# A convolution plus quantised feed-forward kernel: the order of the table work in the lead, regrouped

## The chip, the cores and the metric

The kernel runs on one core of a Trainium2 chip. The metric is the device time of one execution in microseconds (us). Before the change it is 1074.47 us, the median of 3 runs (1073.33, 1074.47 and 1075.77). Engines are named as the profile names them: PE is the matrix engine, DVE the vector engine, ACT the scalar (activation) engine, POOL the general engine, SP the engine that issues most DMAs. L12 means line 12 of the kernel before; the changed kernel's lines are told by the same numbers, so that an operation keeps its name.

## The reference, cut to what matters

The input `x` is (32, 64, 1024): 32 sequences, 64 channels, length 1024. One residual layer is computed:

```python
kernel = _get_kernel(log_dt, C, log_A_real, A_imag, Lq)   # 64 channels x 1024 taps
y = irfft(rfft(u_m) * rfft(kernel))[..., :Lq] + u_m * D   # a causal convolution, plus a skip
cond = y * mask                                           # and a length mask
c2 = cond.reshape(32 * 64, 1024)
gate, up = c2 @ Wg, c2 @ Wu                               # weights of 4 bits, dequantised
out = x + ((gate * sigmoid(gate) * up) @ Wd).reshape(x.shape)   # the product in float16
```

`_get_kernel` is `2 Re sum_n Cs[h,n] exp(dtA[h,n] * l)` over 64 modes `n` for each channel `h` and each tap `l`. The feed-forward contracts over the 1024 positions; its rows are the 2048 pairs of a sequence and a channel, and it has 2752 inner units. So a channel's convolution must be done over all positions before its rows can enter the feed-forward.

## The kernel before, in words

**The taps.** The 1024 taps of a channel are the product of two tables of 32 entries: tap `32a + b` is a sum over 128 rows (64 modes, real and imaginary) of `e1[a] * e2[b]`. The coefficients (decay `na`, phase `wh` and `wl`, amplitude `ab`) come first, for channels 0 to 31 (`head_coefficients`, small DVE instructions of 128x32 and 128x64). Then a group of 4 or 8 channels goes through these steps:

- `decay_tables` (L168): one Exp on ACT per channel, 128x64, into `xd`.
- `phase_tables` (L192 to L204): eight DVE instructions (two products, two roundings, four subtractions), then on ACT two Sin (L207) and two Square (L209). Sin and Exp sit in different table sets of ACT, so an ACT_TABLE_LOAD stands between them.
- `kernel_factors` (L218 to L223): five DVE instructions that make `e2` and `e1`.
- `make_kernel` (L425 to L434): matmuls on PE, one per channel, into `kq`; then `kb`, a high part by ACT (L430) and a low part by DVE (L431), both float16; then two DMAs, issued by ACT (L433), that write them to `kpad` in DRAM.
- `toeplitz` (L525): SP loads, per channel, a 512 KB Toeplitz matrix from `kpad` in overlapping rows.

Groups start at channels 0 and 4 (four channels each), 8, 16 and 24 (eight each). This text says "kernel 8" for the taps of the group that starts at channel 8, and `t0[8]` for the Toeplitz matrix of channel 8.

**The convolution.** `conv_head` makes 24 matmuls (L548) per channel: 8 steps, and in each a high-by-high, a high-by-low and a low-by-high product. Its other operand is the input, cut by `conv_split` (or `conv_load` from channel 16 on) into a float16 high part `uh` (ACT, L495 or L507) and a low part `ul` (DVE, L497 or L510), four channels at a time. After two channels DVE multiplies by the mask (L560), ACT rounds the result to `xh` (L563), and POOL (for channel 15 DVE) makes `xl` (L565). A block is 16 channels, 16 * 32 = 512 rows of the feed-forward, which lie along the free dimension.

**The feed-forward.** `gu_one` and `gu_pair` (L664, L665, L687, L688) multiply `xh` and `xl` with the 4-bit weights, which an unpacker (L578, L579 on SP, L584 on DVE, L590 on POOL, L596 on ACT) prepares; after each group of 128 rows the sums in PSUM are rescaled (L618, L620, L637, L640) by ratios that `scale_ratios` made beforehand (L410 to L418). `dn_pair` (L736, L737) does the down projection.

**What sets the order.** Each engine executes its instructions strictly in the order of its own list. That order is made when the kernel is built: a scheduler places instructions by priority and by its own estimates, and `after(key)` adds the rule that what is issued under it comes after a marked instruction. In the first block (`for i, _ in enumerate(c.conv(0))`, L944) a dictionary `events` issues other work at a given step; eight steps make one channel, so step 7 ends channel 0, step 23 channel 2, step 56 begins channel 7 and so on. `busy(h0, n)` issues `n` matmuls (L891) whose result nobody reads. SP's list is one queue: a load that waits holds up all loads behind it. The SP and ACT DMAs use eight completion semaphores in turn, so a DMA also waits for the eighth one before it.

Of the kernel before, what the change touches and what calls it, by code (L numbers as in the profile page):

```python
# [17 lines left out]
ALU = mybir.AluOpType  # L18
# [164 lines left out]
def phase_tables(nc, side, pool, co, cst, h0, nh):  # L183
# [19 lines left out]
    stt(r1, r1, off1, pl, ALU.subtract, ALU.subtract)  # L203
    stt(r2, r2, off2, pl[:, :, 32:], ALU.subtract, ALU.subtract)  # L204
# [5 lines left out]
    return r1, r2, sq_op  # L210

# [47 lines left out]
class Core:  # L259
# [145 lines left out]
    def scale_ratios(self, s16, nt, g, name, last_factor):  # L405
        nc, keep = self.nc, self.keep
        ratio = keep.tile([128, nt, g - 1], F32, name=name + "r")
        last = keep.tile([128, nt], F32, name=name + "l")
        s, z = self.take([128, nt, g], F32), self.take([128, nt, g], F32)
        nc.scalar.copy(s, s16)  # L410
        for t0, t1, p0, p1, f in last_factor:
            nc.scalar.mul(last[p0:p1, t0:t1], s[p0:p1, t0:t1, g - 1], f)
        nc.vector.tensor_scalar(z, s, 0.0, 2.0 ** -60, ALU.is_equal, ALU.mult)
        nc.vector.tensor_tensor(s, s, z, ALU.add)
        for t0 in range(0, nt, 11):
            t1 = min(nt, t0 + 11)
# [25 lines left out]

    def tables(self, pool, h0, nh):
        held = h0 >= 24
        steps = phase_tables(self.nc, self.nc.vector, pool, self.co, self.cst, h0, nh)
        while True:
            try:
                with self.after("dve" if held else None), self.after("act" if held else None):
                    next(steps)
            except StopIteration as done:  # L450
                self.tab, sq_op = done.value[:2], done.value[2]
                break
            self.dve(800)
            yield
# [36 lines left out]

    def conv_split(self, k, after, last="e"):
        u, uh, ul = self.us[k]
        with self.after(("sq", after)):
            self.nc.scalar.copy(uh, u)  # L495
        with self.after((last, after)):
            self.nc.vector.tensor_tensor(ul, u, uh, ALU.subtract)  # L497
        self.us[k] = uh, ul
# [344 lines left out]
def tile_ssm_ffn(ctx, tc, io):  # L843
# [38 lines left out]
    c.taps(kg, 16)  # L882
    xd = [decay_tables(nc, kg, co, c.cst, h0) for h0 in (0, 8)]
    section(steps)
# [7 lines left out]

    for k, h0 in enumerate((0, 4)):
        every(c.tables(tables, h0, 4))
        every(c.factors(kg, h0, 4, xd[0][:, h0:h0 + 4]))
        c.make_kernel(kg, h0, 4, "b")
        for h in range(h0, h0 + 4):
            c.t0[h] = c.toeplitz(h)
        busy(h0, 8 - 4 * k)
        c.conv_split(k, h0)  # L900
    every(c.tables(kg, 8, 8))
    every(c.factors(kg, 8, 8, xd[1]))
    c.masks()
    tc.no_sync_barrier()
# [22 lines left out]
    def kernel_8():  # L927
        c.make_kernel(kg, 8, 8, "b")
        with c.after("act"):
            xd.extend(decay_tables(nc, kg, co, c.cst, h0) for h0 in (16, 24))  # L930
        for k in (2, 3):
            c.conv_split(k, 8, "kb")
        steps = c.tables(kg, 16, 8)
# [8 lines left out]

    events = {7: kernel_8, 63: lambda: busy(4, 10), 56: ratios_gu, 87: load_16, 75: lambda: c.make_kernel(kg, 16, 8, "b")}
    for i, _ in enumerate(c.conv(0)):  # L944
        if i in events:
            with c.after("dve" if i == 56 else None):
                events[i]()
# [179 lines left out]
```

## Time and profile before

| what | value |
|---|---|
| median of 3 runs | 1074.47 us |
| the profiled execution, its own time | 1075.33 us |
| its span, first to last instruction | 1073.5 us |
| around the span (1075.33 - 1073.5) | 1.8 us |
| PE busy | 1026.2 us, 96% of the span |
| DVE, ACT, POOL busy | 803.7, 775.6, 246.5 us |
| first convolution matmul (L548) starts | 24.53 us |
| last matmul of the first block ends | 58.46 us |
| first feed-forward matmul (L664) starts | 62.15 us |
| DMA, mean | 93 GB/s over the span, 261 GB/s over the first 65 us |

The profile is one execution on the chip. Its second part cuts the span in 40 slices of 26.8 us and gives busy tenths; its fourth follows the chain of waits back from the last instruction; the timeline lists instructions in order of their start, with the idle time of the engine before them and what ended it. "Landed" is the time at which a DMA's semaphore told that it was done. The lead, the subject here, is the first 65 us of 1073.5.

### The profile page before, as it was taken

The page shows a single profiled execution, that of the slowest core. Times are in us where ns is not written, and L with a number is a line of the kernel's source. Part 1 is how long each engine was busy: PE and PEld are TensorE (multiplying, and loading weights), DVE is VectorE, ACT ScalarE, POOL GpSimd, SP SyncE. Part 2 cuts the span into 40 slices and gives each one's busy share as a digit, 9 for nine tenths or more (in the row PEclk, how much of TensorE's full clock was granted, in tenths as well). Part 3 has the DMA queues.
Part 4 walks back from the last instruction along what each step waited for, and adds up shares of the span by engine and source line. Part 5 has one row for each costly group of instructions (what it writes and reads, how often), then busy time and mean ns, then how long its engine had stood idle before and what let it go on. Part 6 is the DMA issues. An engine that isn't in the chain of part 4 may idle for free.

```text
span 1073.5 us, 15382 instructions
## 1 busy us (share of the span) xinstructions
PE 1026.2 (96%) x5854; PEld 513.5 (48%) x5854; DVE 803.7 (75%) x939; ACT 775.6 (72%) x1034; POOL 246.5 (23%) x270
## 2 busy tenths in 40 slices
PE   3989999999999999997999999999999999999996
PEld 2867444444344445663665444444444444444442
DVE  8965788888977786768446777777877777777776
ACT  5767777787677777777577777666666667878775
POOL 0333233232332242231103112221111222102102
PEclk9999999999999999999999999999999999999998
DMA  6976321111111534546753001000000001424102
GB/s 197 331 244 211 101 69 40 40 59 40 42 48 50 143 88 156 164 156 196 231 167 128 30 29 51 20 13 17 20 20 20 20 20 58 129 79 148 59 1 79
DMA packets 52099, 99.76 MB, mean 93 GB/s; under 512 B 9524, under 2 KB 11444, under 8 KB 52024
## 3 DMA queue, kind: packets, MB, share of 16 engines
q1 hardware_dynamic: 38888, 70.09, 20.8%
q0 software_dynamic: 5280, 17.31, 4.3%
q10 hardware_dynamic: 7856, 11.37, 3.6%
q8 instruction: 46, 0.75, 0.3%
q14 instruction: 29, 0.24, 0.1%
HBM read 78.99 MB, written 19.76 MB: 92 GB/s over the span
## 4 chain that ended last, share of the span: by engine, by line
PE 83%; ACT 5%; DMA 4%; DVE 4%; issue 2%; POOL 0%; SPq 0%; DVEq 0%; ACTq 0%
PE chq L687 23%; PE chq L688 22%; PE chq L736 13%; PE chq L737 13%; PE cq L548 6%; PE chq L664 2%; PE chq L665 2%; DMA t<-kpad 2%; ACT chq L640 1%; DVE chq L618 1%; ACT chq L620 1%; DVE v L700 1%; DMA ihl<-kpad 1%; DMA ihl<-xF 1%; PE chq L741 1%
## 5 line engine op out<-in xcount | busy, mean ns | idle before, releaser
L687 PE MATMUL chq<-xh,w 128*128 128x512 f16 x1216 | 460.4, 380 | 5.7 <-DVE chq L618 2.1
L688 PE MATMUL chq<-xl,w 128*128 128x512 f16 x1216 | 458.6, 380 | 0.0
L618 DVE TENSOR_SCALAR chq<-chq,gur 128x1024 f32<-128x1024 f32 x261 | 333.2, 1289 | 95.3 <-PE chq L688 94.1
L620 ACT ACTIVATE chq<-chq,gur 128x1024 f32<-128x1024 f32 x285 | 304.3, 1085 | 86.8 <-PE chq L688 85.5
L640 ACT ACTIVATE chq<-chq,dnr 128x512 f32<-128x512 f32 x372 | 242.1, 661 | 71.7 <-PE chq L737 63.8
L736 PE MATMUL chq<-ihl,wd 128*128 128x512 f16 x672 | 253.8, 380 | 6.5 <-ACT chq L640 3.5
L737 PE MATMUL chq<-ihl,wd 128*128 128x512 f16 x672 | 253.4, 380 | 0.0
L637 DVE TENSOR_TENSOR chq<-chq,dnr 128x1024 f32<-128x1024 f32 x129 | 158.4, 1231 | 83.6 <-PE chq L737 83.2
L688 PEld LDWEIGHTS <-w 128*128 128x128 fp8e4 x1216 | 118.9, 98 | 155.3 <-issue 19.4
L687 PEld LDWEIGHTS <-w 128*128 128x128 fp8e4 x1216 | 118.9, 98 | 145.9 <-issue 1.9
L310 POOL TENSOR_TENSOR ihl<-v,ihl 128x512 f16<-128x512 f32 x42 | 48.3, 1150 | 362.9 <-ACT ihl L629 362.9
L737 PEld LDWEIGHTS <-wd 128*128 128x128 fp8e4 x672 | 65.5, 98 | 76.0 <-issue 12.7
L548 PEld LDWEIGHTS <-t 128*128 128x128 f16 x1152 | 81.4, 98 | 39.2 <-DMA t<-kpad 5.9
L736 PEld LDWEIGHTS <-wd 128*128 128x128 fp8e4 x672 | 65.7, 98 | 67.7 <-issue 1.7
L548 PE MATMUL cq<-uh,t 128*128 128x256 f16 (+3 forms) x720 | 91.8, 226 | 4.6 <-DMA t<-kpad 4.5
L565 POOL TENSOR_TENSOR xl<-y,xh 128x512 f16<-128x512 f32 x28 | 36.2, 1294 | 161.5 <-ACT xh L563 161.5
L548 PE MATMUL cq<-ul,t 128*128 128x256 f16 (+3 forms) x360 | 71.6, 225 | 0.0
L629 ACT CAST ihl<-v 128x512 f16<-128x512 f32 x42 | 25.9, 617 | 58.7 <-DVE v L700 55.3
L700 DVE SCALAR_TENSOR_TENSOR v<-chq,gul,sg 128x1024 f32<-128x1024 f32 x38 | 48.6, 1280 | 17.1 <-PE chq L688 11.3
L310 POOL TENSOR_TENSOR spill<-v,spill 128x512 f16<-128x512 f32 x42 | 48.8, 1161 | 14.2 <-ACT spill L629 13.9
L640 ACT ACTIVATE chq<-chq,gur 128x512 f32<-128x512 f32 x66 | 43.2, 661 | 11.0 <-PE chq L665 9.8
L590 POOL TENSOR_TENSOR w<-w,z 128x256 int32<-128x256 int32 x42 | 31.5, 770 | 82.0 <-DVE w L584 77.6
(250 smaller groups left out, 820.5 us busy)
## 6 DMA issues: line engine op xcount, KB each, us to landing
t<-kpad SPq DMA_DIRECT2D x48, 512.0 KB, 4.4
spill<-spill POOLq DMA_DIRECT2D x42, 256.0 KB, 2.7
ihl<-spill ACTq DMA_DIRECT2D x42, 256.0 KB, 2.8
z<-zc SPq DMA_DIRECT2D x29, 256.0 KB, 3.7
u<-xF SPq DMA_DIRECT2D x12, 512.0 KB, 3.7
xr<-xT SPq DMA_DIRECT2D x12, 512.0 KB, 4.7
out<-xr POOLq DMA_DIRECT2D x24, 256.0 KB, 2.9
w<-qgu SPq DMA_DIRECT2D x21, 256.0 KB, 4.1
```

The costliest lines, as they stand in the source:

```text
L310: self.nc.gpsimd.tensor_tensor(out, a, b, op)
L548: nc.tensor.matmul(q[:, d:, h % 2, :], t0[:, lw, 128 * d:128 * d + 128], uu[:, 0:8 - d, h % 4, :], start=(d == 0 and k == 0 and h % 2 == 0 ...
L565: split.tensor_tensor(xl[:, :, ts], yv, xh[:, :, ts], ALU.subtract)
L618: self.mark("dve", self.nc.vector.tensor_scalar(q, q, col, None, ALU.mult))
L620: self.mark("act", self.nc.scalar.activation(q, q, AF.Copy, scale=col))
L637: self.mark("dve", self.nc.vector.tensor_tensor(q, q, cols.to_broadcast([128, 2, 512]), ALU.mult))
L640: self.mark("act", self.nc.scalar.activation(q[:, k], q[:, k], AF.Copy, scale=cols[:, k]))
L687: nc.tensor.matmul(q[:, b], lw, xh[:, g, :], start=(g == 0), stop=False, skip_group_check=True)
L688: nc.tensor.matmul(q[:, b], lw, xl[:, g, :], start=False, stop=(g == GH - 1), skip_group_check=True)
L700: nc.vector.scalar_tensor_tensor(v, q, last, self.sg.pop(ct - 21), ALU.mult, ALU.mult)
L736: nc.tensor.matmul(qs[j], lw, self.ihl[:, g, 0], start=(g == 0), stop=False, skip_group_check=True)
L737: nc.tensor.matmul(qs[j], lw, self.ihl[:, g, 1], start=False, stop=False, skip_group_check=True)
```

## The change

The diff, cut to its core:

```diff
 # phase_tables also returns the last DVE instruction (L204); tables marks it ("r", h0)
-    def tables(self, pool, h0, nh):
+    def tables(self, pool, h0, nh, key=None):
...
-                with self.after("dve" if held else None), self.after("act" if held else None):
+                with self.after("dve" if held else key), self.after("act" if held else None):
...
+                self.mark(("r", h0), done.value[3])
...
 # scale_ratios
-        nc.scalar.copy(s, s16)
+        with self.after("act"):
+            nc.scalar.copy(s, s16)
...
-    def conv_split(self, k, after, last="e"):
+    def conv_split(self, k, act, dve):
         u, uh, ul = self.us[k]
-        with self.after(("sq", after)):
+        with self.after(act):
             self.nc.scalar.copy(uh, u)
-        with self.after((last, after)):
+        with self.after(dve):
             self.nc.vector.tensor_tensor(ul, u, uh, ALU.subtract)
...
-    xd = [decay_tables(nc, kg, co, c.cst, h0) for h0 in (0, 8)]
+    xd = [decay_tables(nc, kg, co, c.cst, 0)]
...
-    for k, h0 in enumerate((0, 4)):
-        every(c.tables(tables, h0, 4))
+    for h0, fillers in ((0, 8), (4, 2)):
+        every(c.tables(tables, h0, 4, ("e", 0)))
+        if h0 == 0:
+            with c.after(("sq", 0)):
+                xd.append(decay_tables(nc, kg, co, c.cst, 8))
         every(c.factors(kg, h0, 4, xd[0][:, h0:h0 + 4]))
         c.make_kernel(kg, h0, 4, "b")
         for h in range(h0, h0 + 4):
             c.t0[h] = c.toeplitz(h)
-        busy(h0, 8 - 4 * k)
-        c.conv_split(k, h0)
-    every(c.tables(kg, 8, 8))
+        busy(h0, fillers)
+    c.conv_split(0, ("sq", 4), ("e", 4))
+    every(c.tables(kg, 8, 8, ("r", 4)))
+    c.conv_split(1, ("sq", 4), ("r", 8))
     every(c.factors(kg, 8, 8, xd[1]))
-    c.masks()
+    with c.after(("e", 8)):
+        c.masks()
...
     def kernel_8():
         c.make_kernel(kg, 8, 8, "b")
+        for k in (2, 3):
+            c.conv_split(k, "act", ("kb", 8))
         with c.after("act"):
             xd.extend(decay_tables(nc, kg, co, c.cst, h0) for h0 in (16, 24))
-        for k in (2, 3):
-            c.conv_split(k, 8, "kb")
...
-    events = {7: kernel_8, 63: lambda: busy(4, 10), 56: ratios_gu, 87: load_16, 75: lambda: c.make_kernel(kg, 16, 8, "b")}
+    events = {23: kernel_8, 63: lambda: busy(4, 6), 72: ratios_gu, 87: load_16, 66: lambda: c.make_kernel(kg, 16, 8, "b")}
...
-            with c.after("dve" if i == 56 else None):
+            with c.after("dve" if i == 72 else None):
```

In the order that each engine's list takes (read from the two built programs), this does the following. SP's list keeps its order of loads. Behind the first gate-and-up chains, that is from about 80 us of the trace before, all lists are the same.

- DVE: the eight table instructions of group 4 and the first one of group 8 (L192), which stood before the last factor of group 0 (L223), stand behind it; the low parts of the inputs (L497) stand behind the factors of group 4 (channels 0 to 3) and behind the last table instruction of group 8 (channels 4 to 7); the masks (L395, L397, L403) stand behind the factors of group 8; those for channels 8 to 15 behind kernel 8's low part, and the ratios of gate and up (L413 to L418) behind that of kernel 16.
- ACT: eight of the sixteen early Exp move behind the squares of group 0, and with them come one more Exp and one more Sin table load; two input copies (L495) move behind kernel 8's `kb`, and so do the sixteen later Exp, as before; the first of these copies stands between that `kb` and its DMAs. The scale copies (L410, L412) move from before kernel 8's `kb` to behind kernel 16's. One `xh` (L563, channels 0 and 1) stands before kernel 8's `kb`.
- PE: kernel 8's matmuls stand behind channel 2 in place of channel 0; kernel 16's one-channel-per-matmul part (L427) behind the first four matmuls of channel 10 in place of the middle of channel 9; the fillers (L891) number 8, 2 and 6 in place of 8, 4 and 10; the first feed-forward matmul stands behind the first five of channel 17 in place of the seventeenth of channel 16.

More of the change, by code (lines that the diff above doesn't have):

```diff
@@ L203, in phase_tables @@
     stt(r1, r1, off1, pl, ALU.subtract, ALU.subtract)
-    stt(r2, r2, off2, pl[:, :, 32:], ALU.subtract, ALU.subtract)
+    last = stt(r2, r2, off2, pl[:, :, 32:], ALU.subtract, ALU.subtract)
     yield
@@ L209, in phase_tables @@
         sq_op = nc.scalar.activation(r, r, AF.Square, scale=1.4142135623730951)
-    return r1, r2, sq_op
+    return r1, r2, sq_op, last
 def kernel_factors(nc, pool, co, xd, s1, s2, h0, nh):
```

## The prediction

> **What bounds the kernel now.** I read the page's busy rows first, then the busy time in two stretches, before and after 65 us. The columns after the stretch are its length, then the busy time of PE, PEld, DVE, ACT and POOL, the granted clock, the DMA share and GB/s.
>
> ```profile
> 0.00:65.00 65.00, 42.55 (x521) 37.64 (x522) 56.70 (x163) 39.98 (x91) 17.96 (x20) 0.97 0.80 261
> 65.00:1073.50 1008.50, 983.67 (x5336) 475.84 (x5333) 746.97 (x776) 735.59 (x944) 228.51 (x250) 0.99 0.26 82
> ```
>
> Behind the lead PE is busy 97.5% and its list there is not changed. So the change can only move the point from which PE runs full; what it moves there goes to the end one to one. That point is the start of channel 17 at 63.05. The chain of waits up to it (start, length, what):
>
> ```profile
> 10.29 6.90 DMA ihl<-xF
> 17.19 0.29 DVE e1t L223
> ...
> 49.38 0.27 ACT kb L430
> 49.68 0.42 DVE kb L431
> 50.12 5.82 DMA kpad<-kb
> ...
> 56.49 6.50 DMA t<-kpad
> 63.05 0.50 PE cq L548 x3
> ```
>
> Kernel 16's taps are written from 49.67, landed at 55.96, and `t0[17]` landed at 63.0: the last thing that PE waits for. Why `kb` came so late stands in ACT's timeline (start, length; in brackets idle time before):
>
> ```profile
> 30.17 0.36 ACT L430 ACTIVATE kb<-kq 32x256 f16<-32x256 f32 x1
> 30.54 1.28 ACT L168 ACT_TABLE_LOAD   x1
> ...
> 40.87 0.60 ACT L563 CAST xh<-y 128x512 f16<-128x512 f32 x1
> 41.38 2.18 ACT L596 ACTIVATE w<-w,cst 128x1024 fp8e4<-128x1024 uint8 x2
> 46.67 0.62 ACT L563 CAST xh<-y 128x512 f16<-128x512 f32 x1 [3.11 <-DVE y L560]
> 47.20 2.18 ACT L596 ACTIVATE w<-w,cst 128x1024 fp8e4<-128x1024 uint8 x2
> 49.28 0.36 ACT L430 ACTIVATE kb<-kq 32x256 f16<-32x256 f32 x1
> ```
>
> ACT sat 3.11 us for `y` of channels 6 and 7, which on DVE stood behind the ratios, and then did two unpack steps ahead of `kb`. Last, PE in windows of its clock:
>
> ```profile
> 26.13:29.54 3.41, 1.44 (x24) 1.00 0.67 244
> 29.54:32.96 3.42, 3.42 (x29) 0.50 0.83 223
> 56.85:60.27 3.42, 1.61 (x28) 1.00 0.94 248
> ```
>
> After a window with 1.44 us busy the clock was 0.50 for 3.41 us (channels 1 and 2 took 2.76 and 1.92 us; others 1.53, so 1.62 lost); after one with 1.61 it stayed.
>
> **Part by part.** Durations are start-to-start spacings of the rows of before.
>
> Group 0. Nine table instructions leave the way of L223: .34+.34+.26+.20+.33+.20+.39+.26+.60 = 2.92, and L395 .12. They filled gaps of a dependent chain of small instructions; seven such gaps of about .1 open, +.8. Group 0's factor ends at 17.47-3.04+.8 = 15.2; `kb` could follow .73 later (17.47 to 18.20), at 15.95. ACT: squares done at 12.9, then the added Exp load 1.28 and 8 Exp (half of 3.92) 1.96: free at 16.15. So `kb` 0 at 16.2, **-2.0**, and the load of `t0[0]`, 20.46 before, could be issued at 18.5; but input loads run until 18.76 and the write is under them: 18.5 to 19.5, I take 19.0 (-1.5). The fillers stay.
>
> Group 4. Its tables and group 8's first ones now run behind 15.2. DVE: 2.55 for group 4 with `kb`'s low part, 2.47 for five of group 8, 1.9 for the factors: factor end 22.3, before 20.8. ACT: `kb` 16.5, two DMA issues .83, added Sin load 1.28, four functions 1.1: 19.85, in time. Then two input copies 1.98 and a Sin .5: `kb` 4 at 23.0 (22.97 before), its square .5 ahead of the DMAs: written at 23.6 to 23.9, **+.4**. It landed .5 after the queue had run dry (28.5); the queue now runs dry 1.5 earlier, so loads 4 to 7 go at 28.5, before 29.15: **-.6**. The low part of channel 0 (L497) ends at 23.4: channel 0 starts at 23.1, before 24.53. Four fillers less there are free: PE waits.
>
> [...]
>
> Kernel 8. DVE: two low parts 1.13 each, `kb` .2, L204 .4: 25.0; factors 2.05: 27.1, before 28.68. But PE takes channels 1 and 2 first, and ACT has `xh` of channels 0 and 1 ahead of `kb`, which needs the masks (.95) and two tables of group 16 (1.2): `y` 29.05 to 29.75, `xh` 30.35, `kb` 30.4, **+.2**. One input copy (1.0) stands ahead of its DMAs: 31.8, before 30.56, **+1.2**. The wait of PE at 26.76 (1.97) goes. Landing under load took 4.5 (first write of 30.56) to 5.9 (second): loads 8 to 15 go at 36.5 to 38.2, before 37.22; I take 37.5. `t0[8]` landed 5.6 later by the spacing of 1.35 per load before 45.56, at 42.8; PE was with fillers until 44.0. Now 42.6: channels 8 and 9 end at 45.7, before 48.3 with kernel 16's matmuls in them.
>
> Kernel 16. ACT from 30.75: copy 1.0, issues .8, copy 1.0, load 1.28, Exp .3, `xh` .6, 15 Exp 3.6, `xh` .6, load 1.28, four functions 1.77: 43.0, before 40.97. DVE's factors, no longer mixed with ratios: 44.7 (1.9 more if POOL slows them as at 42.04, where L218 took .95 and not .42). `xh` .6 and two unpack steps 2.2: 45.85. Channel 8 and 9's `y` ends at 46.4, `xh` 47.0, one unpack step 1.1, `kb` 48.1, before 49.28: **-1.2**. A copy of scales (.45) precedes the DMAs: 48.9, before 49.67, **-.8**; bounds -1.4 (PE at 44.4, ACT alone) and +.8 (slowed factors). At 5.8 to landing the loads go at 55.2 in place of 56.03. Toward the end PE does channels 10 to 15 until 55.8, before 58.46, and waits for `t0[16]`.
>
> Ratios, scales and masks moved later are hidden: the first rescale is at 64.23, the ratios end near 56, low part `xl` near 60.6 (63.16 before). If that cover went, each us late would be one on PE.
>
> **Sum.** -.8 through kernel 16; a further -.7, because `t0[16]` and `t0[17]` took 4.2 and 6.5 to land from an empty queue (DMA share .27 from 54 to 55, .10 to 55.8, 0 to 57: 2.6 idle) and about a quarter of that gap is now filled by loads that still run; +.2 for one feed-forward matmul that stood ahead of channel 17. **-1.3.** The profiled execution is 1073.5 + 1.8 = 1075.33, so 1074.0; it stands .86 over the median, so by the runs 1074.47-1.3 = **1073.2**. A measurement of this kernel tells about 0.2%, 2.1 us, from no change.
>
> **Rivals.**
>
> 1. *The queue stays full.* If kernel 16's write lands before the loads ahead of it end (about 55.7), 2.1 of the gap of 2.6 goes, and with -1.4 in the chain it is -3.5: 1071.0. For it: loads start 1.5 earlier. Against: kernel 8's write is 1.2 later.
>
> 2. *Slower: kernel 8's write.* Issued at 31.8 and 5.9 to landing, loads 8 to 15 go at 38.2 (+1.0), `t0[8]` at 43.8; fillers end at 40.4, so a clock window has well under 1.44 busy and channels 8 to 10 lose 1.62: `kb` 16 at 50.8 (+1.5). PE waits over 4 us for `t0[16]`, and the feed-forward begins at half clock, 1.62 again: +3.1, 1077.6. It decides as soon as `kb` 16 is later than 49.28. The windows' place is free, so one of the two may be spared (+1.5). For it: six fillers in place of ten. Against: PE's wait at 26.76, which cost the one lost window of before, is gone.
>
>    [...]
>
> 3. *It does little:* ACT's list is the bound, and what DVE gains is waited away: within .5 of before, 1074.5. For it: ACT's work from `kb` 8 to `kb` 16 grows by two copies (2.0) and loses an unpack step (1.1) and the wait (3.1).
>
> **How the numbers follow.** Forecast (-.3 to -2.6 around -1.3): .40, of which .14 lie beyond -2.1. Rival 1: .27, all faster. Rival 2: .22, all but .02 slower. Rival 3: .11, same. Faster .14+.27 = .41, same .26+.02+.11 = .39, slower .20. The range reaches to both rivals, 1070.3 (1071.0 less the .7 that a landing of 4.5 and not 5.2 gives) to 1076.8 (most of rival 2); the likeliest case's own is 1071.9 to 1074.2.
>
> **What would show it.** Group 0's factor at 15.2 and `kb` at 16.2 with Exp ended just before; load of `t0[0]` at 18.5 to 19.5, of `t0[4]` at 28.5, of `t0[8]` at 37.5, of `t0[16]` at 55.2; `kb` 8 at 30.4, `kb` 16 at 48.1; channel 17 at 61.6; no clock of 0.50 after 40 us in the lead. Wrong is it if channel 17 starts within .5 of 63.05, if a second half-clock window shows there, or if the times behind channel 17 do not keep the distance.

## The result, and the profile after

The changed kernel takes 1079.56 us, the median of nine runs (1076.88 to 1080.45), against 1075.05 of nine runs of the kernel before (1073.33 to 1075.9): ratio 1.0039, 95% interval 1.0027 to 1.0051. It is slower, by 4.5 us (0.4%); forecast was 1073.2 and the range ended at 1076.8. Four of the nine lie at 1076.88 to 1077.66, five at 1079.56 to 1080.45; the profiled execution, of the upper ones, took 1079.98 us, with a span of 1078.1 (1073.5 before).

The chain of waits of the changed kernel up to the start of channel 17 (start, length, what; its lines are numbered one or two higher than before):

```profile
31.84 7.43 DMA kpad<-kb
...
39.32 3.77 DMA t<-kpad
...
59.13 6.00 DMA t<-kpad
...
65.17 1.01 PE cq L550 x4
```

The chain has moved: it goes through kernel 8's write, which took 7.43 us to land. The load of `t0[8]` goes out at 39.32 (37.22 before), channel 8 starts at 43.14, channel 17 at 65.17 (63.05 before). PE alone in windows of its clock (stretch, length, busy time, granted clock, DMA share, GB/s):

```profile
39.95:43.36 3.41, 1.01 (x10) 1.00 0.84 204
43.36:46.77 3.41, 3.41 (x22) 0.50 0.95 330
46.77:50.19 3.42, 3.42 (x34) 0.50 1.05 401
60.43:63.84 3.41, 1.16 (x14) 1.00 0.97 243
63.84:67.26 3.42, 2.92 (x23) 0.50 1.05 404
```

The six fillers end at 40.74 and PE stands idle until 43.14. After that window, 1.01 us busy, the clock is 0.50 for two windows (channels 8 to 10), and after one of 1.16 us it is 0.50 again in the first feed-forward. ACT's timeline (in brackets idle time and what ended it):

```profile
29.93 0.62 ACT L565 CAST xh<-y 128x512 f16<-128x512 f32 x1 [4.84 <-DVE y L562]
30.99 0.37 ACT L431 ACTIVATE kb<-kq 32x256 f16<-32x256 f32 x1 [0.45 <-PE kq L428]
...
50.84 0.62 ACT L565 CAST xh<-y 128x512 f16<-128x512 f32 x1 [5.30 <-DVE y L562]
51.36 1.15 ACT L598 ACTIVATE w<-w,cst 128x1024 fp8e4<-128x1024 uint8 x1
52.41 0.36 ACT L431 ACTIVATE kb<-kq 32x256 f16<-32x256 f32 x1
```

`kb` of kernel 8 stands behind `xh` of channels 0 and 1 and comes at 30.99 (30.17 before); `kb` of kernel 16 stands behind `xh` of channels 8 and 9, whose `y` comes late from the slow PE, and an unpack step, at 52.41 (49.28 before).

Set against the profile of before, the same DVE and ACT instructions start 3.11 us later all the way from 70 to 140 us: that is the loss in the lead. From 147 us they are 5.28 later, and 4.63 at the end. The second step stands here, in ACT's timeline, in the DMA view of 142 to 148 us (queue, packets, MB, share of 16 engines; then issues, KB, us to landing), and last in the DMA view of before, 139 to 143 us:

```profile
147.08 0.62 ACT L631 CAST spill<-v 128x512 f16<-128x512 f32 x1 [2.17 <-DMA spill<-spill]
```

```profile
q8 instruction: 1, 0.02, 1.8%
...
spill<-spill POOLq DMA_DIRECT2D x1, 256.0 KB, 4.6
```

```profile
spill<-spill POOLq DMA_DIRECT2D x1, 256.0 KB, 2.4
```

ACT waits 2.17 us for the first store of `spill` to DRAM, since the tile has one buffer. The store took 4.59 us; before it took 2.43. Amid its packets goes one of 16 KB from the queue that the profile calls instruction (q8); it held one of the 16 DMA engines 1.68 us, and the store's last four packets of 4 KB started as it ended. Before, that packet passed at 135.8, in .93 us, ahead of the store.

### The profile page after: what moved, and what is told of

Same layout as the page of the kernel before. It is cut to its first block, busy times and chain, and to the rows that moved or that the text cites. A ratio compares the mean times of both kernels' runs of the same rounds, so it can differ in the third digit from the quotient of the medians.

```text
span 1078.1 us, 15368 instructions
## 1 busy us (share of the span) xinstructions
PE 1027.0 (95%) x5842; PEld 514.2 (48%) x5842; DVE 801.9 (74%) x939; ACT 777.7 (72%) x1036; POOL 244.1 (23%) x270
## 4 chain that ended last, share of the span: by engine, by line
PE 84%; DVE 6%; ACT 4%; DMA 3%; issue 2%; POOL 1%; DVEq 0%; ACTq 0%; POOLq 0%; SPq 0%
PE chq L689 22%; PE chq L690 22%; PE chq L738 13%; PE chq L739 13%; PE cq L550 8%; PE chq L666 2%; PE chq L667 2%; DMA t<-kpad 2%; ACT chq L642 1%; DVE chq L620 1%; DVE v L702 1%; ACT chq L622 1%; DMA kpad<-kb 1%; ACT sg L697 1%; PE chq L743 1%
## 5 line engine op out<-in xcount | busy, mean ns | idle before, releaser
L550 PEld LDWEIGHTS <-t 128*128 128x128 f16 x1152 | 83.8, 100 | 44.7 <-DMA t<-kpad 9.7
L310 POOL TENSOR_TENSOR spill<-v,spill 128x512 f16<-128x512 f32 x42 | 48.7, 1159 | 16.2 <-ACT spill L631 16.1
L642 ACT ACTIVATE chq<-chq,gur 128x512 f32<-128x512 f32 x66 | 43.1, 660 | 9.5 <-PE chq L667 8.4
```

The lines of the kernel that those rows point to most:

```text
L310: self.nc.gpsimd.tensor_tensor(out, a, b, op)
L550: nc.tensor.matmul(q[:, d:, h % 2, :], t0[:, lw, 128 * d:128 * d + 128], uu[:, 0:8 - d, h % 4, :], start=(d == 0 and k == 0 and h % 2 == 0 ...
L642: self.mark("act", self.nc.scalar.activation(q[:, k], q[:, k], AF.Copy, scale=cols[:, k]))
```

## The experiments

**Theories.** Two explanations. A: kernel 8 is late, its write lands behind six loads, PE idles behind too few fillers and loses its clock, kernel 16 follows. B: fewer fillers are fewer PE instructions, so the instruction fetch moves, into the store. Rivals: the regrouping of the first 30 us loses; the fillers lose through the clock alone; the late half loses (ratios at step 72, kernel 16 at step 66).

All kernels beside each other, from their profiles: edits in force, then times in us. "Lead" is how much later than in before the same DVE and ACT instructions start at 75 to 100 us; "xl" the start of DVE's low part of channels 14 and 15; "store" the first `spill` store. R is the regrouping alone. The last columns are the median of 5 to 12 runs, in brackets its distance to the median of before on the same chip (1074.31 to 1075.08 in four series), and the ratio to before with its 95% interval. "Over R" below is a difference of such distances. The ratio is no quotient of these two medians: for a_k8_ratios56 they differ by .9 us. "Lead" isn't the last word on a profile: from 100 to 130 us the same lateness is 3.17 in after_look2, 4.77 in a_fill18, 1.86 in l_late2, 2.80 in l_fill6 and 2.15 in l_fill_end8.

| kernel | kernel 8 at | 16 at | ratios | fillers | load t0[8] | kb 16 | load t0[16] | xl | lead | store | median | ratio, interval |
|---|---|---|---|---|---|---|---|---|---|---|---|---|
| before | 7 | 75 | 56 | 22 | 37.22 | 49.28 | 56.03 | 62.13 | 0 | 2.43 | 1075.05 | 1 |
| changed | 23 | 66 | 72 | 16 | 39.32 | 52.41 | 58.66 | 64.25 | 3.11 | 4.59 | 1079.56 (+4.51) | 1.0039, 1.0027-1.0051 |
| after_look2 | 23 | 66 | 72 | 16 | 39.40 | 51.41 | 58.74 | 63.67 | 2.21 | 4.04 | 1079.74 | one run |
| after_look3 | 23 | 66 | 72 | 16 | 38.93 | 50.74 | 57.94 | 63.00 | 3.83 | 4.31 | 1080.48 | one run |
| a_loads_behind | 23 | 66 | 72 | 16 | 39.24 | 51.29 | 58.16 | 63.55 | 2.43 | 4.33 | 1079.66 (+5.35) | 1.0053, 1.0040-1.0065 |
| a_fill18 | 23 | 66 | 72 | 28 | 39.14 | 47.45 | 56.13 | 64.98 | 3.72 | 2.43 | 1076.62 (+2.31) | 1.0018, 1.0009-1.0028 |
| a_fill_end6 | 23 | 66 | 72 | 22 | 39.63 | 52.70 | 58.86 | 64.96 | 3.23 | 2.43 | 1078.88 (+4.31) | 1.0049, 1.0036-1.0062 |
| a_spill2 | 23 | 66 | 72 | 16 | 39.62 | 49.93 | 57.99 | 62.19 | 2.66 | 4.32 | 1078.85 (+3.80) | 1.0037, 1.0022-1.0051 |
| a_k8_at7 | 7 | 66 | 72 | 16 | 35.50 | 45.80 | 53.13 | 63.48 | 2.22 | 2.83 | 1079.74 (+5.43) | 1.0048, 1.0034-1.0063 |
| a_k8_ratios56 | 7 | 66 | 56 | 16 | 34.37 | 46.57 | 52.92 | 63.00 | 2.28 | 2.72 | 1076.91 (+1.86) | 1.0009, 0.9992-1.0027 |
| R (a_lead_only) | 7 | 75 | 56 | 20 | 33.83 | 47.66 | 54.94 | 60.50 | -1.78 | 2.43 | 1073.78 (-0.53) | 0.9996, 0.9985-1.0007 |
| l_k16_66 | 7 | 66 | 56 | 20 | 36.01 | 46.60 | 55.32 | 61.63 | 0.09 | 2.43 | 1075.35 (+0.27) | 0.9999, 0.9988-1.0010 |
| l_ratios72 | 7 | 75 | 72 | 20 | 37.94 | 47.66 | 56.86 | 62.15 | 1.53 | 2.43 | 1075.23 (+0.15) | 0.9997, 0.9986-1.0008 |
| l_late2 | 7 | 66 | 72 | 20 | 38.24 | 46.88 | 55.56 | 63.78 | 0.84 | 2.43 | 1076.44 (+1.87) | 1.0013, 1.0003-1.0023 |
| l_k8_23 | 23 | 75 | 56 | 20 | 39.59 | 52.22 | 58.50 | 63.60 | 4.03 | 2.44 | 1077.58 (+2.50) | 1.0026, 1.0015-1.0037 |
| l_fill6 | 7 | 75 | 56 | 16 | 37.59 | 47.75 | 56.05 | 60.05 | 2.07 | 4.42 | 1075.58 (+0.50) | 1.0003, 0.9990-1.0016 |
| l_fill_end8 | 7 | 75 | 56 | 28 | 35.09 | 47.83 | 55.18 | 60.67 | 1.20 | 2.44 | 1076.84 (+2.27) | 1.0025, 1.0015-1.0035 |
| b_late_only | 7 | 66 | 72 | 22 | 34.81 | 45.29 | 53.33 | 62.13 | 0.14 | 2.43 | 1078.33 (+3.28) | 1.0027, 1.0014-1.0040 |
| b_late_look2 | 7 | 66 | 72 | 22 | 35.51 | 45.63 | 54.08 | 62.46 | 1.92 | 2.43 | 1076.82 | one run |
| b_fill4 | 7 | 75 | 56 | 16 | 35.47 | 48.90 | 56.17 | 61.74 | 0.39 | 4.39 | 1077.38 (+2.33) | 1.0019, 1.0006-1.0031 |

The names with b_ are the kernel before with an edit, a_ the changed kernel with one undone, l_ R with one added (or fillers behind channel 15).

### Undoing one part at a time

**a_loads_behind**, SP's two input loads held for kernel 8's `kb`:

```diff
+        with self.after(("kb", 8) if h0 == 16 else None):
             self.mark("sp", nc.sync.dma_start(u..., self.io["xF"][h0 // 4]))
-        with self.after("sp"):
+        with self.after("sp"), self.after(("kb", 8)):
             nc.sync.dma_start(raw, ...)
```

> The changed kernel; only SP's loads of channel 16's input (u) and of the unpacker's raw weights are held until kernel 8's low part (kb 8) is done, so that they are issued about when its write is, and no longer ahead of it. Theory A (kernel 8's write is late mostly because six loads stand ahead of it in the DMA queues, and everything in the lead follows from that): the write of 31.84 us, which took 7.43 us to land, takes 5 to 6; load of t0[8] at 37 to 38 (39.32 in the changed kernel), kb 16 at 49.5 to 51 (52.41), start of channel 17 at 62.5 to 63.5 (65.17): 1.5 to 2.5 us faster than the changed kernel. Rival (PE's clock alone: six fillers are too few, whenever the loads come): the landing moves, but PE still idles before channel 8, two half-clock windows stay, kb 16 at 51.5 or later, less than 1 us gained. Rival (kernel 8's kb itself, .8 late, sets the rest): nothing gained, since kb 8 stays at 31. The weights that are now loaded later are needed by the first unpack step: if ACT waits for them, the gain is eaten there, and a row with ACT waiting for a DMA shows it.

The edit did not do what it was made for: `after` only orders the program, and SP issued both loads at 30.84 and 31.48, still ahead of the write (32.35). Nothing was gained and nothing is told of the loads: no run here tests them alone.

**a_fill18**, `busy(4, 6)` to `busy(4, 18)`:

> The changed kernel with eighteen filler matmuls ahead of channel 8 in place of six. Theory A: the load of t0[8] stays at 39.3 and channel 8 cannot start before about 43; eighteen fillers last 4.7 us from 39.2, to about 43.9, so PE has no idle window there, channels 8 to 10 run at full clock, kb 16 comes at about 50.5 to 51 (52.41), and channel 17 begins 1 to 1.9 us earlier than 65.17: time between the changed kernel and before, 1 to 2 us faster than the changed one. Rival (the fillers alone make the loss): as before the change, within .5 us, with kb 16 at 49.3. Rival (ACT and DVE are the bound in that stretch, PE's clock is covered): kb 16 stays at 52.4, nothing gained. Theory B (part of the loss, 2.16 us at 142 to 147 us, is one 16 KB instruction fetch that falls into the first spill store, and its place in time depends on how many PE instructions came before): twelve more PE instructions move that fetch some 4 to 5 us earlier, to about 139 us, clear of the store, so the store lands in 2.4 us in place of 4.6 and a further 2.2 us are gained; without B the store stays as it is.

No half clock ahead of channel 10, and `kb` 16 at 47.45, five us earlier: yet the lead ended .6 later still, xl at 64.98. So with the clock kept and kernel 16 early, something else holds the end of the lead, and theory A does not say what. The store took 2.43, as B says, and the distance to before is 2.2 smaller than the changed kernel's. The profile is the slowest of the eleven runs (1078.22, median 1076.62), so the late lead need not be the median's.

**a_k8_at7**, in `events` `23: kernel_8` to `7: kernel_8`:

> The changed kernel with kernel 8 made at the early place of the kernel before (step 7 of the first channels, not 23), so that its matmuls stand ahead of channel 1 on PE and its kb ahead of every xh on ACT. Theory A with the rival that kernel 8's own lateness is the cause: kb 8 at 29.5 to 30.2 (30.99), its write issued at 30 to 30.9 in place of 31.39 and 31.84, so ahead of or amid the loads of u and the raw weights, landed by 36 to 37.3, load of t0[8] at 36.5 to 37.3 (39.32), kb 16 at 49 to 50, channel 17 at 62.5 to 63.5 (65.17): 1.5 to 2.7 us faster than the changed kernel. Rival (the loads ahead of the write alone): the write still lands 7 us after its issue, t0[8] at 38.3 or later, gain under 1 us. Rival (PE's clock alone): two half-clock windows stay before channel 10 and kb 16 at 51.5 or later.

Kernel 8's write (28.76) and the load of `t0[8]` (35.50) came a us earlier than expected, and `kb` 16 even 3.5 us ahead of before. The lead was still 2.22 late and the median no better. DVE was busy without a gap from 48.2 to the `y` of channels 14 and 15 at 61.45, though PE had ended channel 15 at 57.2. This is in a profile that is the fastest of its five runs (1076.63, median 1079.74). That made theory C: the ratios, now in this stretch, hold up DVE.

**a_k8_ratios56**, the ratios put back as well:

```diff
-    events = {23: kernel_8, ..., 72: ratios_gu, ...
-            with c.after("dve" if i == 72 else None):
+    events = {7: kernel_8, ..., 56: ratios_gu, ...
+            with c.after("dve" if i == 56 else None):
 # and the scale copy without after("act")
```

> The changed kernel with two things put back: kernel 8 at step 7 and the ratios of the gate and up scales at step 56, without the order behind ACT. Six fillers and kernel 16 at step 66 stay. The runs with kernel 8 alone put back, and with eighteen fillers, had kb 16 at 45.80 and 47.45 us (49.28 before) and still ended the lead 2.2 and 3.7 us later than before; so the late kernel 16 of theory A does not set the end. New theory C: the ratios at step 72 put about 3.6 us of DVE (row groups of lines 414 to 419) between the y of channels 8, 9 and that of channels 14, 15, a stretch in which DVE has no idle time; y(14,15) comes at 61.5 though PE had channel 15 done at 57.2, its xh at 62.9, the low part xl at 63.5, and the feed-forward waits for them. By C: y(14,15) at 57.5 to 59, xl at 59.5 to 60.8, end of the lead 1 to 2.2 us earlier than before, 1073 to 1074.5 us. Rival A (fillers: PE idles before channel 8, half clock): lead later than before by 1 us or more, 1076 us or more. Rival (kernel 16's early place makes loss by itself): y(14,15) still at 61 or later.

C's numbers did not come: `y` of 14 and 15 at 61.50, not 57.5 to 59. PE's timeline shows another wait in its place, and the windows what it cost:

```profile
45.15 1.06 PE L427 MATMUL kq<-e2t,e1t 128*32 128x32 f32 x16 [2.93 <-DVE e1t L223]
```

```profile
40.41:43.82 3.41, 1.81 (x18) 1.00 1.05 392
43.82:47.24 3.42, 2.09 (x27) 0.50 1.05 388
```

Kernel 16's matmuls, at step 66, stand in the middle of channel 8 and wait from 42.2 for DVE's factor, which the ratios now delay; PE loses its clock with them (theory D). The distance to before is 2.7 smaller than the changed kernel's; the interval does not tell it from nothing.

### The regrouping alone, and one edit on it

**a_lead_only**, called R:

```diff
-    events = {23: kernel_8, 63: lambda: busy(4, 6), 72: ratios_gu, 87: load_16, 66: ...
+    events = {7: kernel_8, 63: lambda: busy(4, 10), 56: ratios_gu, 87: load_16, 75: ...
 # and the scale copy without after("act")
```

> Only the regrouping of the lead's first 30 us from the change (tables wait for the factors ahead, fillers 8 and 2, input copies and masks later); kernel 8 at step 7, ten fillers at step 63, ratios at step 56 and kernel 16 at step 75 as in the kernel before. Theory A (the regrouping is sound by itself; what loses is kernel 8's place and the few fillers): factor 0 at 15.4, t0[0] at 19.6, kb 8 at 30.2 or earlier, t0[8] at 36.5 to 37.5, one half-clock window in the lead less than the changed kernel, channel 17 at 62 to 63.3: within 1 us of the kernel before, on either side. Rival (the regrouping itself costs: two more table loads on ACT and loads that go out earlier than the write): t0[8] at 38.5 or later also here, channel 17 at 64 or later, 1.5 to 3 us slower than before. Theory B (instruction fetch in the spill store): ten fillers at step 63 and six fewer ahead move the fetch by some 2 us toward the store, from 135.8 to about 138; the store at about 139 to 141 may or may not meet it; where it does, 2.2 us more, and the runs fall into two groups.

The regrouping loses nothing: in the profile its lead ends 1.78 earlier than before (which lost a window at half clock there, R none), in the median it gains .5 us, which the interval does not tell from nothing. So the rest of the change is the loss, and it can be added edit by edit.

**l_k16_66**, `75:` to `66:` for kernel 16:

> The kernel with only the lead's regrouping (its lead ended 1.78 us earlier than before; call it R), plus one edit of the change: kernel 16 at step 66 in place of 75. DVE's list is the same as in R; on PE kernel 16's matmuls move ahead by nine steps of channel 8. Theory D: at step 66 PE arrives at about 43.4, but DVE's factor 16 (line 223) ends at 45.1 in R: PE stands there 1.5 to 2 us with channel 8 unfinished, that clock window is busy near the point where it halves (1.44 of 3.41 halved, 1.61 did not), and y(8,9) comes at 49.5 to 50.5 in place of 48.39. kb 16 comes at 46.0 to 46.6 (47.66). Lead 0 to 3 us later than R, 1074 to 1077 us. Rival (an earlier kernel 16 is a gain, as predicted): t0[16] earlier by 1 us or more, lead as R or earlier, 1073 to 1074 us.

PE waited for the factor (.88 us, less than the 1.5 to 2 expected) but kept its clock there (2.54 us busy in 43.34 to 46.76, at 1.00 there and in the next window). The cost came later, in PE's wait for `t0[16]`. R's windows of the clock and this kernel's, PE alone:

```profile
55.07:58.48 3.41, 1.76 (x32) 1.00 0.66 195
58.48:61.90 3.42, 2.79 (x30) 1.00 1.01 328
```

```profile
57.00:60.41 3.41, 0.96 (x17) 1.00 1.01 275
60.41:63.82 3.41, 3.41 (x26) 0.50 1.06 410
```

R's wait (56.8 to 58.96) falls on the edge of two windows, which keep 1.76 and 2.79 us of work, and the clock stays at 1.00; here it lies within one, which keeps .96, and the feed-forward begins at half clock. The windows begin at another time in R (55.07) than here (57.00), so part of this is chance. "Kernel 16 earlier" did not bring an earlier `t0[16]`: its write, issued 1.1 earlier, landed at 55.23 (54.85 in R), behind the same loads. In the median +.8 over R, inside the uncertainty.

**l_ratios72**, ratios at step 72 behind ACT:

> R (lead regrouping only) plus one edit of the change: the ratios of the gate and up scales at step 72 behind ACT in place of step 56. Theory C: factor 16 on DVE is no longer mixed with ratios and ends 1 to 2 us earlier than 45.1, kb 16 at 46.5 to 47.5; but 3.6 us of ratios then lie between y(8,9) and y(14,15), which comes at 59.5 to 61.5 (58.55 in R), xl 61.5 to 63 (60.50): lead 1 to 2.3 us later than R, 1074.5 to 1076.5 us. Rival (that stretch has room, the feed-forward waits for t0[16] and the unpacked weights anyway): lead within .5 of R, 1073.3 to 1074.3 us.

xl came 1.65 later than in R, as C says. A second cost was not expected: the reciprocals stand ahead of kernel 16's own low part on DVE, so the second half of its write was issued only at 52.05 and `t0[16]` at 56.86. DVE's timeline:

```profile
48.89 2.33 DVE L418 RECIPROCAL ihl<-ihl 128x88 f32<-128x88 f32 x4
51.14 0.35 DVE L432 SCALAR_TENSOR_TENSOR kb<-kq,kb 32x256 f16<-32x256 f32 x1
```

In the median +.7 over R, inside the uncertainty.

**l_late2**, both of these on R:

> R (lead regrouping only) plus both late edits of the change: ratios at step 72 behind ACT, kernel 16 at step 66; kernel 8 at step 7 and ten fillers as in R. If the two cost together (as the median of the kernel before with both, +2.9 us, says): y(14,15) at 60 to 61.5 (58.55 in R), xl at 62 to 63.5, lead 2 us or more later than R, 1075.8 to 1077.8 us. If each is neutral and they stay so together: y(14,15) below 60, 1073.5 to 1075.5 us. The first spill store takes 2.43 by theory B, with 20 fillers, in both cases.

Together they cost: 2.4 over R, and xl is what is late (PE waits for `xh` and then for xl), although the load of `t0[16]` is earlier than before and no window behind 40 us is at half clock. xl in DVE's timeline of R, then `y` and xl in that of this kernel:

```profile
60.50 1.03 DVE L566 TENSOR_TENSOR xl<-y,xh 128x512 f16<-128x512 f32 x1
```

```profile
61.75 0.68 DVE L562 TENSOR_TENSOR y<-cq,mask 128x512 f32<-128x512 f32 x1
...
63.78 1.07 DVE L567 TENSOR_TENSOR xl<-y,xh 128x512 f16<-128x512 f32 x1 [0.96 <-ACT xh L565]
```

ACT's timeline of this kernel shows what came last, and it is not `y`, which C named:

```profile
61.57 1.15 ACT L598 ACTIVATE w<-w,cst 128x1024 fp8e4<-128x1024 uint8 x1 [3.12 <-POOL w L592]
...
63.15 0.60 ACT L565 CAST xh<-y 128x512 f16<-128x512 f32 x1
```

`y` was done at 62.43, .7 us before `xh` began. In ACT's list an unpack step stands ahead of `xh`; it waits 3.12 us for POOL's step (60.38), which starts as DVE's (L586, 58.92 to 60.29) ends, and that stands behind the ratios, as `y` does. ACT waits for POOL in the same place in the profiles of the changed kernel, a_k8_at7, l_ratios72 and b_late_look2 (2.86 to 3.89 us). So C has the engine right, and the link runs through the unpack steps; that the ratios alone make DVE's step late is not shown, since the scheduler also ordered DVE's other work anew.

**b_late_only** and **b_late_look2**, the same two edits on the kernel before:

> The kernel before with only the second half of the change: ratios at step 72 behind ACT, kernel 16 at step 66; the first 30 us, kernel 8 and the fillers as before. Theory C (the ratios fill DVE ahead of y(14,15)): kb 16 no later than 49.3, y(14,15) at 61 to 62.5 in place of 60.18, xl at 63 to 64.5 in place of 62.13, lead 1 to 3 us later than before, 1075.5 to 1077.5 us. Theory A (only the landing of kernel 8's write and the clock in 40 to 50 us lose): no loss here, kb 16 up to 2 us earlier, 1073 to 1074.5 us.

> A second look at the kernel before with the two late edits (ratios at step 72, kernel 16 at step 66), whose first profiled execution was the fastest of twelve (1074.01 us; median 1078.33). If the loss is in the lead: y(14,15) at 61 or later and lead 2 to 4 us later than before in an execution near 1078. If it is a collision of a fetch with a store: lead within .5 of before, and a store on the path that takes 4 us or more. An execution near 1074 again would leave it open.

The median says +3.3, more than C expected. The first profile was the fastest of its twelve runs and shows no loss (`y` of 14 and 15 at 59.78); the second, 1.5 us below the median, has that `y` at 60.12, short of the 61 expected, and the lead 1.92 late with the feed-forward at half clock (0.76 and 0.74 in 60.43 to 67.26), waiting 2.74 us for `xh` of channels 14 and 15. That is a loss in the lead, as C says, with the clock's on top; the first store is short, so it is no collision with a fetch.

**l_k8_23**, kernel 8 at step 23 on R:

> R (lead regrouping only) plus one edit of the change: kernel 8 at step 23 in place of 7. Theory A: kb 8 at 31 or later, its write issued behind the loads of t0[4] to t0[7] and of the next inputs and 6 to 7.5 us to landing, load of t0[8] at 38.3 to 39.5 (33.83 in R), channel 8 at 42.5 to 43.5 (42.15 in R, behind ten fillers), kb 16 at 49 to 52, t0[16] at 57 to 59: lead 2 to 4.5 us later than R, 1075.5 to 1078.5 us. Rival (kernel 8's place matters little, since the fillers cover it): lead within .7 of R, 1073 to 1074.5 us.

The one edit of the change that costs clearly by itself: 3.0 over R (ratio 1.0026, interval 1.0015 to 1.0037). What A names is there: write issued at 31.36 and 32.15, `t0[8]` at 39.59, channel 8 at 43.60, `kb` 16 at 52.22, half clock at channel 8 and in the feed-forward (0.50 in 44.38 to 47.80 and in 61.45 to 68.28). But the chain of waits up to channel 8 goes through ACT:

```profile
43.06 0.52 ACT xh L564
43.58 0.02 issue
43.60 4.38 PE cq L549 x36
```

`t0[8]` took 3.77 us in the changed kernel; by that it landed here at about 43.4 (an estimate), so two waits end close together, and ACT's list, late since kernel 8, is a rival to the write that no run separates: the event at step 23 also carries the input copies, the later Exp and the first tables of group 16. Over all kernels, kernel 8 at step 23 put the load of `t0[8]` at 38.93 to 39.63 in eight executions; at step 7 it lay at 33.83 to 38.24 in twelve.

**l_fill6**, `busy(4, 10)` to `busy(4, 6)` on R:

> R (lead regrouping only) plus one edit of the change: six fillers at step 63 in place of ten. t0[8] is the gate of channel 8 at 42.1 in R, behind fillers that end at 41.7. With six they end at 40.8, and PE idles 1.3 us more: window 39.9 to 43.4 falls from 2.96 busy to about 2.4 to 2.6, above the 1.61 that kept full clock. Expected by theories C and D: lead within .4 of R. Theory A's clock part (fillers alone decide): a half-clock window, lead 1 to 1.8 us later. Theory B (each filler fewer moves the instruction fetch by about 1 us toward the first spill store: 2 fewer fillers moved it 2.2 us against the lead, 6 fewer 5.9): fetch, 136.5 in R, to 140 to 141, first store (issued 137.8, done 140.23 in R) just missed or met, and the time 0 to 2 us above R without any change of the lead.

The lead did not stay: `t0[16]` was loaded at 56.05, the window 54.95 to 58.36 had 1.43 us of work (R's, nearly the same window, 1.76), and the clock was 0.50 for 6.8 us. This profile is the slowest of twelve runs (1080.41); the median is 1.0 over R. B came as expected: store 4.42.

### The fetch and the store

**b_fill4**, `busy(4, 10)` to `busy(4, 4)` on the kernel before, and **a_spill2**, `bufs=1` to `bufs=2` for the tile "spill" of the changed kernel:

> The kernel before with four fillers ahead of channel 8 in place of ten: six PE matmuls fewer, nothing else. Theory B (an instruction fetch of 16 KB moves with the number of PE instructions, by about .4 to 1 us per filler in the runs so far, and delays the first spill store when it falls into it): the fetch at 135.8 us moves to 139 to 141.5, the store issued at about 139.3 takes 2.6 to 4.8 us in place of 2.43, and the distance to the kernel before grows by .5 to 2.2 us at 140 to 147 us; runs in two groups, median 1 to 2.2 us above before. Rival (the long store has another cause): store at 2.3 to 2.5 as before. The lead itself: t0[8] had landed near 42.8 while the fillers lasted until 44.0, so by the row it may gain up to 1 us at channel 8, or lose 1.6 if the clock halves.

> The changed kernel with two buffers in place of one for the tile that is stored to DRAM as spill, so that ACT's next copy into it does not wait for the store. Theory B: the lead ends as late as in the changed kernel (+3.1), but the second step of +2.16 at 142 to 147 us is gone wherever the fetch falls; runs at 1076.5 to 1077.7 and no second group at 1080; median 2 to 2.5 below the changed kernel. Rival (the two groups come from something else than this store): two groups stay, median within 1 us of 1079.6.

b_fill4's lead is .39 late; at 140 to 150 us its lateness rises from .59 to 2.57. Its DMA view of 139 to 145 us:

```profile
q8 instruction: 1, 0.02, 1.0%
...
spill<-spill POOLq DMA_DIRECT2D x1, 256.0 KB, 4.4
```

In a_spill2 the store is as long (4.32) but the step shrinks to under .5 us, since ACT goes on in the other buffer. Over all 20 executions the place of the fetch goes by the number of fillers: 28 put it 5.7 to 6.0 us ahead of the store's issue, 22 3.0 to 3.5, 20 1.0 to 1.3, and 16 put it 1.5 to 2.4 us behind. The 11 executions with 20, 22 or 28 fillers have stores of 2.43 or 2.44; the nine with 16 have 4.04 to 4.59 seven times, 2.72 and 2.83 twice. B is shown for the store. For the runs' times B failed: a_spill2 gained only .7 us on the changed kernel in the median, not 2 to 2.5, and its runs still lie in two groups (four at 1077.31 to 1078.12, four at 1079.57 to 1081.44), as the rival said. So ACT's wait for that store is not what parts the two groups, and how much of the 4.5 it makes over many executions is not shown.

**a_fill_end6**, six fillers behind channel 15 of the changed kernel, and **l_fill_end8**, eight on R:

```diff
-    events = {..., 87: load_16, ...
+    events = {..., 87: load_16, 127: lambda: busy(4, 6), ...   # 8 on R
```

> The changed kernel plus six fillers behind channel 15 (step 127), where its PE waits 2.63 us for t0[16] (60.05 to 62.68); they last 1.5 us and delay nothing ahead of them, so t0[8], kb 8, kb 16 and the first two half-clock windows stay as in the changed kernel. Theory B (count of PE instructions): 22 fillers in all, as before the change, so the fetch lies about 3.5 us ahead of the first spill store, which takes 2.4 to 2.5 us in place of 4.59: 2.2 us gained. The window that halved the clock at 63.84 (1.16 busy in 60.43 to 63.84) gets 1.5 more and stays full: up to 1.6 us more. Together 1075.8 to 1077.5 us, against 1079.56. Rival (the place of the fillers counts, not their number): store 4.3 to 4.6, 1078 us or more.

> R (lead regrouping only) plus eight fillers behind channel 15 (step 127), where PE waits 2.13 us for t0[16] in R (56.8 to 58.96); eight fillers last 2.0 us. In R the window 57.02 to 60.43 was 1.47 us busy and kept full clock; in the runs where t0[16] came later (kernel 16 at step 66: .96 busy, six fillers: 0 busy) the feed-forward began at half clock and the lead ended 1.9 and 3.9 us later than R. With the fillers no window at 57 to 64 us halves whatever the landing, and 28 fillers in all put the instruction fetch some 5 us ahead of the first spill store. Expected: lead as R or up to .5 later by the fillers themselves, spread of the runs smaller, median 1072.5 to 1073.8 us, 1 to 2 us faster than before. Rival (clock windows there are not what varies): median as R, 1073.5 to 1074.5 us, same spread.

a_fill_end6 brought the store back to 2.43 and took away the third half clock (1.00 in 63.32 to 66.73), but the lead stayed 3.23 late, with xl at 64.96, and the distance to before is only .2 smaller than the changed kernel's: 1078.88, where B expected 1077.5 at most. It is the number of fillers that moves the fetch, not their place (22 put it 3.0 to 3.5 us ahead of the store also with six of them behind channel 15); the gain of 2.2 us did not come. l_fill_end8 is a miss, 2.8 over R: with the fillers the order made by the scheduler changed too, the feed-forward of channels 14 and 15 moved ahead of channel 16, PE waited 1.80 us for its `xh`, and the window 57.95 to 61.37, 1.53 us busy, halved the clock all the same.

**after_look2** and **after_look3**, the changed kernel again:

> The changed kernel as it is, a second look. Theory B: near 1077 us the first spill store (4.59 us in the first look) takes 2.3 to 3.0 us and the lead is 3.1 late as before; near 1080 it takes 4 to 4.8 again. Rival (the lead itself varies): store 4 us or more in both groups, and channel 17 starts 1.5 us or more before 65.17 in an execution near 1077.

> The changed kernel as it is, a third look, with the same expectations as the second: near 1077 us a store of 2.3 to 3.0 us with the lead 3.1 late (theory B), or a store of 4 us or more with channel 17 1.5 us earlier or more (rival: the lead varies); near 1080 us store 4 to 4.8 and channel 17 near 65.2.

Both fell into the upper group, with long stores and the lead late again (by 2.21 and 3.83); kernel 8's first write took 6.96 and 6.76 to land. In after_look3 `kb` 16 came 1.7 earlier than in the first profile of this kernel and the lead ended .7 later. What the runs near 1077 do otherwise stays open.

No version beat both kernels: R is faster than the changed kernel (0.9996 against 1.0039) and not to be told from before.

## Why the prediction was wrong

- **Groups 0 and 4: right but for channel 0.** Factor 0 ended at 15.44 (forecast 15.2), `kb` 0 came at 16.20 (16.2), the load of `t0[0]` at 19.58 (19.0), `kb` 4 at 22.96 (23.0), the load of `t0[4]` at 28.67 (28.5). The added table loads cost their 1.28 and nothing behind: the one from 12.98 is followed by its Exp at 14.27, the one from 17.46 by its Sin at 18.76. Channel 0 started at 24.07, not 23.1. R shows that this part is no loss.
- **Kernel 8: the first step that failed.** "Landing under load took 4.5 to 5.9": it took 6.5 and 7.4. The bound was read from a write that was issued amid the loads of `t0[6]` and `t0[7]`; the change issues it behind all of them and the two input loads. `kb` 8 was .8 late, not .2. The load of `t0[8]` at 39.32 lies outside both bounds (36.5 to 38.2). l_k8_23 shows that this edit alone costs 3.0 over R. The sum slipped here too: by its own 5.6 from load to landing a load at 37.5 lands at 43.1, not 42.6.
- **The ratios: "hidden".** The cover was counted to the first rescale, but nearer work stands behind them in DVE's list: its unpack step, for which POOL and then ACT wait ahead of `xh` of channels 14 and 15, and the `y` of these channels. Low part xl came at 64.25, not "near 60.6", and l_late2 shows it with an early `t0[16]`.
- **Kernel 16: 48.1, measured 52.41.** Worse than the number is the link: "-.8 through kernel 16" took it that an earlier `kb` brings an earlier end. In a_k8_at7 it was 3.5 earlier than before and the lead 2.2 later; at step 66 PE waits for the factor, and in l_k16_66 a write issued 1.1 earlier than in R landed .4 later.
- **The fillers.** "Free" was said of those ahead of channel 0. Those ahead of channel 8, six for ten, had no term in the sum: with fillers ending at 40.4 and `t0[8]` at 42.6 PE idles 2.2 us, and only rival 2 asked what that does to the clock (2.40 us measured, and two windows at 0.50). Nor did any term have their count: sixteen in all move the instruction fetch into the first store.
- **Rival 2**, with a chance of .22, named the place, the clock and the sign. It priced the loss at 3.1 and the profile has 3.11 in the lead; that these agree is luck, since the terms differ (two windows lost at channel 8, not one, PE's wait for `t0[16]` 2.63 us, not over 4, and DVE's late xl). Its 1077.6 already lay beyond the range. The second step of 2.2 us at 142 us, which no rival had, comes on top in the profiled execution; a_fill_end6 lost as much in the median with a short store.
- **Named signs.** Channel 17 late, half-clock windows behind 40 us and a distance that isn't kept behind channel 17: all three came.

Added up from the medians over R: kernel 8 at 23 3.0, the two late edits together 2.4, six fillers 1.0, against 5.0 for the changed kernel over R (4.51 + .53). Each has an uncertainty of some 1.7 us (two intervals of 1.2), and the waits lie beside each other, so the sum of 6.4 is no contradiction; the shares cannot be told finer. So kernel 8's place and the two late edits are shown to cost; which wait in them makes how much is argued from single profiles. Two late chains that end near one another also fit what undoing kernel 8 alone showed: `kb` 16 came early, xl was late, and nothing was gained.

## What to carry to other kernels

Where two chains meet close to the end of a stretch, take every edit back and add them to the good version, one by one and then together (each late edit alone stayed inside the uncertainty, both cost 2.4); undoing one of them on the bad version can show nothing. Price a small DRAM write by what is in the queues when it will be issued, not by how long the same write took before (kernel 8's first one took 3.2 to 5.1 us behind one or two loads, 6.2 to 7.2 behind four; that the loads are the cause is not shown). Read more than one execution where a half-clock window hangs on some tenths of a microsecond (1.53 us of work was followed by one, 1.61 twice by none): the profile of b_late_only was the fastest of its twelve runs, that of l_fill6 the slowest.

## What the runs showed of the hardware

- A 16 KB packet of the instruction queue held one DMA engine .88 to 1.78 us (46 of them in the profile of before, 45 in that of the changed kernel). Where one fell into the first 256 KB store, that took 4.04 to 4.59 us in seven of nine executions and 2.72 and 2.83 in two, in place of 2.43 or 2.44.
- The clock's windows, set on the edges that the trace shows: from 20 us on, in the leads of the 20 executions, every window of 3.41 us with 1.53 us of PE work or less was followed by a clock of 0.50 (27 of them); of sixteen at full clock with 1.6 to 2.1 two were (1.81 in a_k8_ratios56 and 1.85 in a_loads_behind). The busiest of the 27 had 1.53 of 3.41 us of work, 45% (l_fill_end8). The half clock lasted one window, two or once three; what decides it is not shown. The windows' place differs from run to run: one begins at 55.07 in R and at 57.00 in l_k16_66.
- Kernel 8's first write took 3.2 to 7.2 us to land, with the same bytes: 3.47 in R (issued at 29.01), 6.91 in l_ratios72 (issued at 28.89), both amid the loads of `t0[4]` to `t0[7]`. It goes with how many of these four loads had been issued ahead of it: behind one or two it took 3.2 to 5.1 (seven executions, R with two), behind three 4.5 to 6.9 (four, l_ratios72 among them), behind all four 6.2 to 7.2 (nine: l_late2 and the eight with kernel 8 at step 23). That the loads are the cause is not shown by an edit.
